# Four images through two attention layers and two Mamba layers: the last MLP of each image, the reload of x, and a softplus one slot later

## The chip, the cores and the metric

One NeuronCore of a Trainium2 chip runs the whole program. The metric is device time in microseconds (us). The kernel before took 12309.68 us in the median of three runs (12303.26 to 12313.59).

The engines are named as in the profile: PE multiplies matrices (PEld loads its weights), DVE and POOL work elementwise, ACT evaluates functions from a loaded table, and SP issues DMAs. Each engine takes its instructions in the order in which they were written and waits for others by semaphores.

## The reference

x is 4 images of 256 channels and 64 x 64 places. Four layers each add their result to x after a group normalisation (32 groups):

```python
x = x + L0(_gn(x))   # gated scan over rows, then window attention
x = x + L1(_gn(x))   # the same with other weights
x = x + L2(_gn(x))   # layer norm, Mamba with 512 inner channels, 16 states
x = x + L3(_gn(x))   # 4 groups of 64 channels, Mamba with 128 inner channels each, MLP, 1x1 convolution
```

What matters here is the end of L3, for every group of 64 channels, and the softplus in L2:

```python
m = _ln(m, ln1_g, ln1_b)                                   # m: output of the Mamba of one group
m = gelu(m @ fc1_w + fc1_b, approximate=False) @ fc2_w + fc2_b
m = m + skip_scale * ch
xo = m.reshape(4, b, N, D).transpose(1, 3, 0, 2).reshape(b, C, H, W)
y = einsum('oc,bchw->bohw', outc_w, xo)                    # then batch norm: scale and bias per channel
return silu(y)
...
delta = softplus(einsum('blr,dr->bld', dt, dt_proj_w) + dt_proj_b)   # in L2's Mamba
```

## The kernel before, in words

`net_kernel` (L1924) runs the images one after the other. For each it takes the x tile (128 partitions, two halves of 4096 columns, 4 MB), loads both halves (L1932), and calls `attention_layers` for L0 and L1, `mamba_layer` for L2 and `grouped_mamba_layer` for L3. x stays in the on-chip memory between the layers. The first thing that L0 does with it is a sum over a strip of eight columns (`gn_s`, L145); a strip has all 64 rows, so it reaches through the whole tile. Before it, DVE prepares small constants from the loaded vectors `att_v` (L107).

Both Mamba layers cut the 4096 places of an image into 4 chunks of 1024 and each chunk into 4 blocks (in L2 128 of the 512 channels, in L3 one group, of which two form a pair c). `scan_blocks` (L800 to L944) goes through all blocks; a block has 16 slots, one per state n. In a slot, DVE multiplies `pb` by `du` (L912) and scans (`h`, L918), POOL multiplies by C (`hc`, L924), ACT makes a later slot's decay (`da`, L854), SP loads a later slot's C row (`cb`, L818, three slots ahead, four buffers), PE spreads a later slot's B row into `pb` (L842) and turns the products of the slot before into the sum `y` (L870). In a few slots (0, 5, 10 in L2; 0, 4, 8 in L3) B comes by DMA instead (`bb`, L824, one buffer), POOL multiplies it by `du` (L828) and the decay goes to PSUM (`dap`). After a block, `end` copies `y` into `du` (L881), turns it back and adds the D term on PE (`fin_ps`, L891, L895), and multiplies by the gate (`m_zs`, L884); this happens in slots 1 to 3 of the next block, and after the last block at once.

All other work is put by hand into slots: `put(block, (slots), steps)` appends steps to a block's slots, and they run on their engines after that slot's scan and products. A slot's place in the code thus sets its order on every engine's queue.

- `x_proj` makes the B, C and step rows of a block (`table_steps`, L1058 to L1090): products on PE, an eviction to `bct` on ACT, two DMAs of B and C rows to memory, and then four correction steps (ACT L1079, POOL L1082, ACT, POOL) which split B for the spreading.
- `delta` makes the softplus of a block (`delta_steps`): `dt_ps` on PE (L1039), Abs, Exp and Ln on ACT (L1041 to L1043), an addition on DVE (L1047), each twice, then `du` on POOL (L1051).
- In L2, these run for the next chunk's first block in the last block of a chunk (L1399, L1400): projections in slots 7, 8, 8, 9, corrections in 9 to 12, softplus in 9, 10, 10, 11 and `du` in 12.
- In L3, `mlp(k, c, s)` (L1633) is the MLP of half s (512 places) of pair c of chunk k, seven steps: output product and its square and copy (L1640 to L1646), variance and inverse root (L1650, L952, L953), multiplication on POOL (L1655), first MLP product (L1661), two Gelus with the second product between, after which ACT's table for Exp and Ln is loaded again (L1668, L948), and the second product with the skip term in two steps (L1684, L1689, L1694). A pair's two halves run in the slots of the next pair; what does not fit goes to the pair after that (`late`).
- `out_conv` (L1709, L1715) makes the 1x1 convolution with the batch norm, `out_silu` (L1728) the Silu of a chunk's four pieces, and `out` (L1734, L1735) adds x on POOL and writes the piece to memory.

After the last scan (L1905 to L1920) the code runs the late steps of pair (3, 0), second half; then both halves of the last pair's MLP, first three steps in turn, then the first half to its end and the second half to its end; then four convolutions, one Silu pass, four additions with four output DMAs. PSUM's pool "mm" has two banks of 512 columns and serves all of these products; the pool "pb" has two buffers of 1024.

The table load for Gelu or Silu is its own ACT instruction, put in where the next function is not in the loaded set.

Of the kernel before, what the change touches and what calls it, by code (L numbers as in the profile page):

```python
# [8 lines left out]
F32 = mybir.dt.float32  # L9
# [9 lines left out]
P = 128  # L19
# [25 lines left out]
class Net:  # L45
# [1067 lines left out]
    def mamba_layer(self, x, bridge, pe_dram, w_in, w_cw, w_x, w_dt, w_out, v_dram):  # L1113
        tc, nc = self.tc, self.nc
        ND = 4
        with ExitStack() as ctx:
# [148 lines left out]
            def delta(k, d):  # L1265
                return self.delta_steps(
                    chunks[k]["blocks"][d], wdt[:, d * P : (d + 1) * P], work, psum
                )
# [76 lines left out]
            for k in range(n_chunk):  # L1345
                more = k + 1 < n_chunk
                bg = [blk["bg"] for blk in chunks[k]["blocks"]]

                def put(d, where, steps):
                    for i, f in zip(where, steps):  # L1350
                        bg[d].setdefault(i, []).append(f)

                if k == 0:
                    put(0, (2, 3, 4, 5), folds)
                if k:
                    for i, where in enumerate(((3, 4, 5), (6, 7, 8), (9, 10, 11), (12, 13, 14))):
                        put(0, where, out_proj(k - 1, i // 2, i % 2))
                put(0, (9, 10, 11, 12, 12), delta(k, 1))
                put(0, (14, 15), (in_z(k, 0, 0), in_z(k, 0, 1)))
                put(1, (1,), (silu((k, 0, "zs")),))  # L1360
                put(1, (6, 7, 8, 9, 10), delta(k, 2))
                put(1, (11, 12), (in_z(k, 1, 0), in_z(k, 1, 1)))
                put(1, (14,), (silu((k, 1, "zs")),))
                at = (6, 7, 8, 9, 10) if more else (5, 6, 7, 8, 9)
                put(2, at, delta(k, 3))
                at = (10, 11) if more else (8, 9)
                put(2, at, (in_z(k, 2, 0), in_z(k, 2, 1)))
                z3 = in_z(k, 3, 0), in_z(k, 3, 1)
                if more:
                    put(3, (0, 1), z3)  # L1370
                else:
                    put(2, (10, 11), z3)
                if more:

                    if k == 0:
                        put(0, (0,), (lambda: begin(1),))
                        put(0, (0, 0, 1, 3, 4, 5, 6, 7), self.later(lambda: norm(1, 0), 8))
                    h1 = self.later(lambda k=k: norm(k + 1, 1), 8)
                    if k:
                        put(0, (2, 4, 5, 7, 8, 13, 14, 15), h1)  # L1380
                    else:
                        put(0, (7, 8, 9, 12, 13, 14, 15), h1[:7])
                        put(1, (1,), h1[7:])
                    if k + 2 < n_chunk:
                        put(3, (3,), (lambda k=k: begin(k + 2),))
                        h0 = self.later(lambda k=k: norm(k + 2, 0), 8)
                        put(3, (4, 6, 7, 14, 15), h0[:5])
                        chunks[k + 1]["late"] = ((0, 1, 2), h0[5:])
                    if k:
                        put(0, *chunks[k]["late"])  # L1390
                    u = all_u(k + 1)
                    put(1, range(5, 16), u[:11])
                    put(2, range(14), u[11:25])
                    put(3, (1, 2, 3, 4, 5, 5, 6), u[25:])
                    xs = x_proj(k + 1)
                    put(2, (13,), (silu((k + 1, 0, "u"), (k + 1, 1, "u"), (k + 1, 2, "u"),
                                        (k, 2, "zs")),))
                    put(3, (7,), (silu((k + 1, 3, "u"), (k, 3, "zs")),))
                    put(3, (7, 8, 8, 9, 9, 10, 11, 12), xs)  # L1399
                    put(3, (9, 10, 10, 11, 12), delta(k + 1, 0))  # L1400
                else:
                    put(2, (13,), (silu((k, 2, "zs"), (k, 3, "zs")),))

                    sums, about, square, squares, early_squares = stats

                    def square_into(i):
                        tag, bufs = ("pe", 1) if i % 2 else ("u", 5)
                        square(i, work.tile([P, NC], F32, tag=tag, name="cs_sq", bufs=bufs))

                    for i in range(6):  # L1410
                        put(1 + (13 + i) // DS, ((13 + i) % DS,), (lambda i=i: sums(i),))
                        put(2 + (12 + i) // DS, ((12 + i) % DS,), (lambda i=i: square_into(i),))
                        put(2 + (13 + i) // DS, ((13 + i) % DS,), (lambda i=i: squares(i),))
                    put(2, (3,), (about,))
                    put(3, (3,), (early_squares,))
                    for i in range(4):
                        at = (6 + 2 * i, 7 + 2 * i)
                        put(3, at, out_proj(k, i // 2, i % 2, ((0, 1, 2),)))
# [67 lines left out]
        return [step(i) for i in range(n)]  # L1486


    def grouped_mamba_layer(self, x, bridge, begun, ws_dram, outc_dram, v_dram, out_b):
        tc, nc = self.tc, self.nc  # L1490
        w_in, w_cw, w_x, w_dt, w_out, w_f1, w_f2 = ws_dram
        with ExitStack() as ctx:
# [209 lines left out]
                )  # L1702


            def out_conv(k, s, m):
                def step():
                    ps = psum.tile([P, NT], F32, tag="mm", name="oc_ps")
                    for c in range(2):
                        nc.tensor.matmul(  # L1709
                            ps, woc[:, c, m * P : (m + 1) * P],  # L1710
                            chunks[k]["xo", c][:, s : s + NT], start=(c == 0), stop=(c == 1),
                        )
                    if s == 0 and m == 0:
                        chunks[k]["yo"] = work.tile([P, 4, NT], F32, tag="hid", name="yo", bufs=1)
                    nc.scalar.activation(  # L1715
                        yo(k, s, m), ps, AF.Identity, bias=bnb[:, m : m + 1], scale=bns[:, m : m + 1]
                    )

                return step
# [7 lines left out]
                for sm in outs:  # L1727
                    nc.scalar.activation(yo(k, *sm), yo(k, *sm), AF.Silu)  # L1728

            def out(k, s, m):  # L1730
                def step():
                    t0 = k * NC + s
                    xs = x[:, m * T + t0 : m * T + t0 + NT]
                    nc.gpsimd.tensor_tensor(yo(k, s, m), xs, yo(k, s, m), ALU.add)  # L1734
                    nc.sync.dma_start(out_b[m * P : (m + 1) * P, t0 : t0 + NT], yo(k, s, m))  # L1735

                return step
# [112 lines left out]
            for i, (k, c) in enumerate(pairs):  # L1850
# [19 lines left out]
                if i:  # L1870
                    m0, m1 = mlp(*pairs[i - 1], 0), mlp(*pairs[i - 1], 1)
                    put(even, (5, 6, 7, 10, 11, 12, 13), m0)
                    put(even, (6, 7, 8), m1)
                    if c == 0:
                        put(even, (14, 15), m1[3:])
                        put(odd, (0, 1), m1[5:])
                    else:
                        put(odd, (15,), m1[3:])
                        late.append(((0, 1, 1), m1[4:]))
                put(even, (7, 8, 8, 9, 10), delta(k, 2 * c + 1))  # L1880
                also = [lambda k=k: out_silu(k - 1)] if c == 1 and k else []
                if i == 0:
# [4 lines left out]
                put(even, (3,), (silu(k, c, "zs", also),))  # L1887
                if c == 1 and k:
                    put(even, (4, 4, 5, 5), [out(k - 1, *sm) for sm in outs])
                if c == 0 and k:  # L1890
                    put(odd, (10, 12, 15), [out_conv(k - 1, *sm) for sm in outs[:3]])
                    late.append(((0,), [out_conv(k - 1, *outs[3])]))
# [9 lines left out]
                [blk for c in chunks for blk in c["blocks"]], loop, psum, psb, psy, (0, 4, 8),  # L1902
                (1, 2, 2), (xs0[2:4], (), xs0[4:]),
            )
            k = n_chunk - 1  # L1905
            for _, steps in late:
                for f in steps:
                    f()
            tail = [mlp(k, 1, 0), mlp(k, 1, 1)]
            for i in range(3):  # L1910
                for fs in tail:
                    fs[i]()
            for fs in tail:
                for f in fs[3:]:
                    f()
            for sm in outs:
                out_conv(k, *sm)()
            out_silu(k)
            for sm in outs:
                out(k, *sm)()  # L1920


@with_exitstack
def net_kernel(ctx, tc, a, out):  # L1924
    net = Net(tc, ctx)
    nc = tc.nc
    xp = ctx.enter_context(tc.tile_pool(name="x", bufs=1))
    x_dram = a["x"]
    for b in range(NB):
        x = xp.tile([P, 2 * T], F32, name="x")  # L1930
        for c in range(2):
            nc.sync.dma_start(x[:, c * T : (c + 1) * T], x_dram[b, c * P : (c + 1) * P, :])  # L1932
        net.attention_layers(
            x, [a[f"l{i}_w"] for i in range(2)], [a[f"l{i}_v"] for i in range(2)]
        )
        with tc.tile_pool(name="bridge", bufs=1, reuse_waits="tile") as bridge:
# [3 lines left out]
            )  # L1940
            net.grouped_mamba_layer(
                x, bridge, begun, [a[f"m3_{k}"] for k in ("in", "cw", "x", "dt", "out", "f1", "f2")],
                a["m3_oc"], a["m3_v"], out[b],
            )


# [81 lines left out]
```

## Time and profile before

| what | us |
|---|---|
| median of three runs | 12309.68 |
| profiled execution, its own time | 12326.55 |
| its span | 12324.8 |
| x loads of the four images issued at | 0.75, 3083.27, 6161.24, 9240.05 |
| image 0: attention, first Mamba, grouped Mamba | about 992, 1039, 1052 |
| busy: PE, DVE, POOL, ACT | 9979.3, 9877.7, 8959.7, 7059.2 |
| granted PE clock, mean over the span | 0.916 |

The profile is of one execution. Its timeline lists instructions with start, duration, engine, line, what they write and read, and in brackets how long the engine stood idle before and who ended that. The chain of waits follows the end back from step to step, and its rows give start, duration and the step; "issue" is time for which no wait is seen. The windows view gives, for a stretch of time, the busy time of PE, PEld, DVE, ACT and POOL (with the number of instructions), then the granted clock of PE (1.00 is full), the share of time in which the DMA engines were busy, and GB/s.

### The profile page before, as it was taken

To read this page: it belongs to the slowest core of one execution; us is meant where nothing else is said; L and a number is where in the kernel's file an instruction comes from. 1 tells how busy PE (TensorE), PEld (TensorE's weight loads), DVE (VectorE), ACT (ScalarE), POOL (GpSimd) and SP (SyncE) were. 2 spreads that over 40 slices of the span, in tenths; PEclk is the share of its full clock that TensorE was granted. 3 is DMA by queue.
4 is the path that set the end of the run, shared out by engine and by line. 5 is a ranking of instruction groups with operands and counts; after the bars stand their busy time and mean duration, and the time that the engine had idled before them with its cause. 6 is when DMAs were issued, how large, how long until landed. Compare 5 with 4: busy or idle time off the path is not lost.

```text
span 12324.8 us, 191425 instructions
## 1 busy us (share of the span) xinstructions
PE 9979.3 (81%) x70976; PEld 5673.2 (46%) x70976; DVE 9877.7 (80%) x8362; ACT 7059.2 (57%) x13044; POOL 8959.7 (73%) x4570
## 2 busy tenths in 40 slices
PE   7887887777788788777788878877778887887777
PEld 4554444443455444444345544444434554444443
DVE  6667998897666799889766679988976667998887
ACT  4555555776455555577545555557754555555775
POOL 3666886887366688688736668868873666886887
PEclk9998998998899899899889989989988998998998
DMA  2344554554334455455433445545542344554554
GB/s 90 103 122 133 168 173 144 168 168 142 93 102 122 133 168 173 144 169 170 141 91 102 123 135 169 172 145 167 170 142 89 102 123 135 169 172 144 167 170 140
DMA packets 680421, 1742.03 MB, mean 141 GB/s; under 512 B 89120, under 2 KB 195120, under 8 KB 678464
## 3 DMA queue, kind: packets, MB, share of 16 engines
q1 hardware_dynamic: 679488, 1729.78, 43.8%
q8 instruction: 562, 9.21, 0.3%
q14 instruction: 371, 3.04, 0.1%
HBM read 1601.51 MB, written 94.37 MB: 138 GB/s over the span
## 4 chain that ended last, share of the span: by engine, by line
DVE 33%; PE 33%; ACT 16%; issue 9%; POOL 6%; DMA 2%; SPq 2%; DVEq 0%; POOLq 0%; ACTq 0%
DVE h L918 16%; PE conv_ps L204 7%; DVE pb L912 7%; PE y L870 5%; PE u_ps L1205 3%; ACT pr L501 3%; ACT da L854 2%; PE pb L842 2%; DVE lp L240 2%; PE sc L480 2%; DVE mn L490 2%; PE u_ps L1572 2%; SPq L456 1%; POOL pr L515 1%; DMA kv<-kv_dram 1%
## 5 line engine op out<-in xcount | busy, mean ns | idle before, releaser
L924 POOL TENSOR_TENSOR hc<-h,cb 128x1024 f32<-128x1024 f32 x2056 | 4815.6, 2351 | 965.0 <-DVE h L918 416.4
L918 DVE TENSOR_TENSOR_SCAN h<-da,m_state,pb 128x1024 f32<-128x1024 f32 x1248 | 2919.8, 2340 | 159.7 <-POOL bb L828 1.0
L870 PE MATMUL y<-ident,hc 128*128 128x128 f32 x16384 | 2371.7, 293 | 345.7 <-POOL hc L924 272.0
L870 PEld LDWEIGHTS y<-ident,hc 128*128 128x128 f32 x16384 | 2093.4, 152 | 1011.6 <-POOL hc L924 447.2
L912 DVE TENSOR_TENSOR pb<-du,pb 128x1024 f32<-128x1024 f32 x1672 | 2024.5, 1211 | 95.6 <-PE pb L842 92.8
L854 ACT ACTIVATE da<-delta,m_v 128x1024 f32<-128x1024 f32 x1672 | 1898.8, 1141 | 221.0 <-DVE h L918 204.2
L842 PE MATMUL pb<-m_parts,pick 128*128 128x512 bf16 x3312 | 1098.1, 416 | 871.4 <-DVE h L918 818.0
L501 ACT ACTIVATE pr<-sc,mn 128x256 f32<-128x256 f32 x2048 | 958.0, 490 | 773.0 <-DVE mn L490 555.3
L515 POOL TENSOR_TENSOR pr<-pr,sm 128x1024 f32<-128x1024 f32 x512 | 967.3, 1899 | 457.8 <-DVE sm L513 359.7
L842 PEld LDWEIGHTS <-pick 128*128 128x128 bf16 x3312 | 255.6, 101 | 1880.0 <-DVE h L918 1155.4
L918 DVE TENSOR_TENSOR_SCAN h<-da,pb 128x1024 f32<-128x1024 f32 x424 | 969.5, 2287 | 54.0 <-DVE pb L912 0.5
L828 POOL TENSOR_TENSOR bb<-du,bb 128x1024 f32<-128x1024 f32 x376 | 889.4, 2365 | 79.7 <-DMA bb<-m_cd 71.3
L490 DVE TENSOR_REDUCE mn<-sc 128x4 f32<-128x1024 f32 x512 | 609.7, 1219 | 386.0 <-PE sc L480 386.0
L529 PE MATMUL pt_ps<-ident,pr 128*128 128x128 f32 x4096 | 592.0, 290 | 219.6 <-ACT pts L542 136.9
L918 DVE TENSOR_TENSOR_SCAN h<-dap,m_state,bb 128x1024 f32<-128x1024 f32 x288 | 672.0, 2333 | 76.1 <-ACT dap L854 63.0
L204 PE MATMUL conv_ps<-att_y,att_wb 128*128 128x512 f32 x1536 | 692.8, 595 | 4.4 <-DVE gn_mean L151 4.4
L529 PEld LDWEIGHTS pt_ps<-ident,pr 128*128 128x128 f32 x4096 | 474.1, 147 | 432.9 <-issue 192.4
L854 ACT ACTIVATE dap<-delta,m_v 128x1024 f32<-128x1024 f32 x376 | 419.5, 1116 | 416.9 <-DVE h L918 318.4
L480 PE MATMUL sc<-kv,q 32*64 32x128 f32 x16384 | 410.5, 300 | 151.5 <-DMA kv<-kv_dram 94.9
L555 PE MATMUL ov_ps<-pts,kv 128*32 128x64 f32 x16384 | 432.4, 234 | 112.4 <-DVE pts L540 65.4
L240 DVE SCALAR_TENSOR_TENSOR lp<-vimg,att_v,lp 128x512 f32<-128x512 f32 x616 | 465.5, 756 | 27.9 <-DVE lp L240 0.5
L859 ACT ACTIVATE m_state<-h 128x1 f32<-128x1 f32 x1536 | 290.6, 192 | 344.2 <-DVE h L918 343.5
(269 smaller groups left out, 17409.3 us busy)
## 6 DMA issues: line engine op xcount, KB each, us to landing
cb<-m_cd SPq DMA_DIRECT2D x2048, 512.0 KB
kv<-kv_dram SPq DMA_DIRECT2D x2048, 128.0 KB
bb<-m_cd SPq DMA_DIRECT2D x376, 512.0 KB
kv_dram<-kst SPq DMA_DIRECT2D x128, 256.0 KB
kv_dram<-vn SPq DMA_DIRECT2D x128, 256.0 KB
q<-q SPq DMA_DIRECT2D x256, 128.0 KB
x<-in_x_dram SPq DMA_DIRECT2D x8, 2048.0 KB
m_pe<-in_pe_dram SPq DMA_DIRECT2D x32, 512.0 KB
```

The costliest lines, as they stand in the source:

```text
L204: nc.tensor.matmul(ps, w[:, k, w0 + m * P : w0 + (m + 1) * P], src[:, k], start=(k == 0), stop=(k == 1),)
L490: nc.vector.tensor_reduce(mn[h], sc[h].rearrange("p r w m n -> p (w m) r n"), AX.XY, ALU.min)
L501: nc.scalar.activation(t[:, g].rearrange("p j r t -> p r j t"), sc[h][:, :, g // 2, g % 2, :].rearrange("p r (j t) -> p r j t", j=2), AF.E ...
L515: nc.gpsimd.tensor_tensor(t, t, s.rearrange("p (a o) -> p a o", o=1).to_broadcast([P, 4, 256]), ALU.mult,)
L529: nc.tensor.transpose(pt[h][j][:, g, :], t[:, g, j].rearrange("p r t -> p (r t)"), self.ident,)
L828: nc.gpsimd.tensor_tensor(pb[i], slots[i][0]["du"], pb[i], ALU.mult)
L842: nc.tensor.matmul(pb[i][:, ss], self.pick[:, n : n + 1].to_broadcast([P, P]), blk["parts"][:, ss], start=True, stop=True,)
L854: nc.scalar.activation(da[i], blk["delta"], AF.Exp, scale=blk["a"](n))
L870: nc.tensor.matmul(blk["y"][:, ss], t[:, ss], self.ident, is_transpose=True, start=(n == 0 and ss.start % NT == 0), stop=(n == DS - 1 and ...
L912: nc.vector.tensor_tensor(pb[i], blk["du"], pb[i], ALU.mult)
L918: nc.vector.tensor_tensor_scan(h[i][:, ss], da[i][:, ss], pb[i][:, ss], state, ALU.mult, ALU.add)
L924: nc.gpsimd.tensor_tensor(hc[i][:, ss], h[i][:, ss], cb[i][:, ss], ALU.mult)
```

## The change

Four things change, in three functions.

1. L2: the four correction steps go from slots 9 to 12 to slots 10 to 13, and the next block's softplus from slots 9, 10, 10, 11 (and 12 for `du`) to 10, 11, 11, 12, 12, and is written ahead of the corrections in a slot they share.
2. L3, last pair: the leftover steps of the second half of pair (3, 0) run in slots 3 to 6 of the last block instead of after the scan.
3. L3, after the scan: both halves of the last MLP go together. All the output products, squares and copies come first, then both inverse roots, with the multiplication on DVE; the first MLP product of both groups goes into one "pb" buffer and one Gelu takes it at 1024 columns; no table load lies between the halves; the Gelus' results go into free buffers of `delta` and `du`. The Silu reads the convolution's PSUM bank directly, with batch norm's scale and bias, and the addition of x is on DVE, piece by piece.
4. x is one tile for all images. Chunk k - 1 of the next image is loaded (1 MB) in slot 8 of the first block of pair (k, 1), after that chunk's output additions in slots 4 and 5; chunk 3 after the last output. Only the first image is still loaded at once.

```diff
-                    put(3, (7, 8, 8, 9, 9, 10, 11, 12), xs)
-                    put(3, (9, 10, 10, 11, 12), delta(k + 1, 0))
+                    put(3, (7, 8, 8, 9), xs)
+                    put(3, (10, 11, 11, 12, 12), delta(k + 1, 0))
+                    put(3, (10, 11, 12, 13), xs[4:])
...
-            def out_conv(k, s, m):
+            def out_conv(k, s, m, func=AF.Identity):
...
-                        yo(k, s, m), ps, AF.Identity, bias=bnb[:, m : m + 1], scale=bns[:, m : m + 1]
+                        yo(k, s, m), ps, func, bias=bnb[:, m : m + 1], scale=bns[:, m : m + 1]
...
-            def out(k, s, m):
+            def out(k, s, m, eng=nc.gpsimd):
...
-                    nc.gpsimd.tensor_tensor(yo(k, s, m), xs, yo(k, s, m), ALU.add)
+                    eng.tensor_tensor(yo(k, s, m), xs, yo(k, s, m), ALU.add)
...
-                    else:
+                    elif i + 1 < len(pairs):
                         put(odd, (15,), m1[3:])
                         late.append(((0, 1, 1), m1[4:]))
+                    else:
+                        put(odd, (3, 4, 5, 6), m1[3:])
...
+                    put(even, (8,), [lambda k=k: load(slice((k - 1) * NC, k * NC))])
...
-            for _, steps in late:
-                for f in steps:
-                    f()
-            tail = [mlp(k, 1, 0), mlp(k, 1, 1)]
...
+            k, pair = n_chunk - 1, chunks[-1]["blocks"][2:]
+            sq = [work.tile([P, 2, NT], F32, tag="sq", name="m_sq") for s in range(2)]
+            for s in range(2):
...
+                nc.scalar.activation(sq[s][:, 0, :], ps, AF.Square)
+                nc.scalar.activation(sq[s][:, 1, :], ps, AF.Copy)
+            for s in range(2):
...
+                self.rsqrt(sq[s][:, 0, :], pv, self.eps)
+                nc.vector.tensor_tensor(sq[s][:, 1, :], sq[s][:, 1, :], sq[s][:, 0, :], ALU.mult)
+            hid = {}
+            for s in range(2):
+                for f in range(2):
+                    ps = psb.tile([P, 2, NT], F32, tag="pb", name="f1_ps")
...
+                    nc.scalar.activation(hid[s, f], ps, AF.Gelu, bias=f1b[:, f : f + 1])
...
+            for s in (0, NT):
+                for m in range(2):
+                    out_conv(k, s, m, AF.Silu)()
+                    out(k, s, m, nc.vector)()
+            load(slice(k * NC, T))
...
+    x = xp.tile([P, 2 * T], F32, name="x")
+
+    def load(b, ts):
+        if b < NB:
+            nc.sync.dma_start(
+                x.rearrange("p (c t) -> p c t", c=2)[:, :, ts], x_dram[b][:, :, ts]
+            )
```

## The prediction

> **What bounds the kernel now.** I read the sum first. The profiled execution took 12326.55 us with a span of 12324.8, and the three timed runs have a median of 12309.68; the sum below is made against the profiled execution and its gain is then taken from the median. The four x loads start at 0.75, 3083.27, 6161.24 and 9240.05 us, so one image takes about 3080 us and every edit is paid four times (the reload three times, the first Mamba layer's shift twelve).
>
> The page's busy shares (PE 81%, DVE 80%, POOL 73%) are averages and say little here, so the next view is the chain of waits over the boundary between image 0 and image 1, in order of time (start, us, what):
>
> ```profile
> 3028.04 2.53 POOL hc L924 x2
> 3030.56 18.29 issue
> 3048.89 1.28 POOL m_sq L1655
> ...
> 3067.99 7.08 PE oc_ps L1709 x16
> ...
> 3075.89 1.28 ACT L1728
> ...
> 3077.89 4.94 POOL yo L1734 x4
> ...
> 3084.24 12.23 DMA att_v<-in_l_v_dram
> 3096.97 2.25 DVE gn_s L145 x2
> ```
>
> The last scan product ends at 3030.57. From there to the x load at 3083.27 lie 52.7 us of small dependent steps, with no other work beside them; then 13.6 us of pure loading until DVE's first reduction at 3096.88. The same stretch is 53.2 us in images 1 and 2 and, up to the last addition, 54.7 us in image 3. So about 66 us per image boundary have one thing running at a time.
>
> Two rows of the timeline show why even the scan's own last step is late. The Gelu of a leftover MLP half takes its table load here, and holds both "mm" banks that the scan's `fin_ps` needs:
>
> ```profile
> 3032.45 1.28 ACT L1668 ACT_TABLE_LOAD   x1
> 3033.74 1.27 ACT L1668 ACTIVATE hid<-f_ps,m_f1b 128x512 f32<-128x512 f32 x2
> 3034.48 0.71 PEld L891 LDWEIGHTS fin_ps<-ident,du 128*128 128x128 f32 x4 [3.45 <-ACT hid L1668]
> ```
>
> The windows view gives PE's busy time first and the granted clock third from last:
>
> ```profile
> 3027.00:3032.00 5.00, 2.40 (x16) 1.69 (x16) 2.18 (x2) 0.64 (x2) 3.37 (x3) 1.00 0.00 2
> 3032.00:3037.00 5.00, 2.52 (x6) 1.48 (x7) 0.00 (x0) 2.99 (x4) 0.00 (x0) 0.50 0.00 0
> 3047.00:3052.00 5.00, 2.59 (x7) 0.60 (x6) 0.00 (x0) 4.72 (x8) 2.50 (x2) 1.00 0.00 0
> 3052.00:3057.00 5.00, 4.89 (x8) 1.59 (x10) 0.00 (x0) 3.30 (x5) 0.00 (x0) 0.55 0.00 0
> ```
>
> Twice PE is half idle for five us, and in the next five its clock is half. In the tail the clock is a cost of its own.
>
> For the first Mamba layer I read DVE's timeline in the last block of the third chunk, and POOL's in that of the second:
>
> ```profile
> 1753.09 2.33 DVE L918 TENSOR_TENSOR_SCAN h<-dap,m_state,bb 128x1024 f32<-128x1024 f32 x1
> 1758.52 0.69 DVE L1047 SCALAR_TENSOR_TENSOR delta<-dt_ps,delta 128x512 f32<-128x512 f32 x1 [3.10 <-ACT delta L1043]
> ```
> ```profile
> 1522.22 2.12 POOL L1082 TENSOR_TENSOR m_bct<-m_bct,m_parts 64x1024 f32<-64x1024 f32 x1
> 1524.31 2.35 POOL L924 TENSOR_TENSOR hc<-h,cb 128x1024 f32<-128x1024 f32 x1
> 1528.13 2.36 POOL L924 TENSOR_TENSOR hc<-h,cb 128x1024 f32<-128x1024 f32 x1 [1.47 <-issue]
> ```
>
> DVE stands still for the softplus: 2.02, 1.86 and 3.10 us at the three chunk ends, 2.04, 1.85 and 3.11 in the other images: 7.0 us per image, 28 in all. POOL idles only 1.45 and 1.47 us in the same stretch of the first two.
>
> **Part 1, the tail.** I rebuild it from the same rows, once with PE at full clock and once at half, starting from 3030.57. In brackets: full / half.
> - The leftover half is gone from here, so `fin_ps` starts when the first `du` copy ends (3031.9, not 3034.5). Transposes and diagonal product twice, then the second 0.69 us multiply: ends 3035.2 / 3037.7 (before 3040.2).
> - `m_ps`, Square and Copy: PE to first Square 1.1 to 2.2, then ACT's four took 2.12 from 3045.16: ends 3037.7 / 3042.1.
> - Ln and Exp for both halves 2.58 (3047.47 to 3050.05); the multiply goes from POOL (1.28) to DVE (0.69 by L1287's and L884's rows) and hides under the Gelu table's 1.28: first Gelu 3041.9 / 3046.5.
> - Four Gelus of 128x1024 instead of eight of 128x512. No row shows this op at that width; L854 of the same size takes 1.14, so four are 4.6, and PE's two 64-row products between them add nothing at full clock (1.16 to the evicting op, row 3050.21) and about 2 in all at half: ends 3046.4 / 3053.2.
> - `f2_ps` twice: from skip product to `xo` 3.07 at full clock (3064.99 to 3068.06), 5.3 at half (3054.69 to 3060.00), the first partly under the last Gelu; `xo` ends 3051.6 / 3060.4.
> - `oc_ps` is paced by PE, 16 matmuls in 7.1. Silu is read from PSUM, so its table load (1.28) fits under PE's first pair, the separate Silu pass (2.19) goes, and the four POOL additions (4.93 on the path) become DVE additions of which only the last 0.69 shows. `oc_ps` starts under the last `xo`, so last addition 7.9 after it at full clock, 8.2 at half.
>
> The x load is then issued at about 3060 / 3069, not 3083.27. PE has no gap above 2.5 us in this tail but is half idle around Ln/Exp, which is what preceded half clock before; I take 3063: 20 us per image in images 0 to 2 and 22 in image 3, where the tail before was 2 longer. **Tail: -83** (ends -57 and -97). Where a stall goes, the next one late is PE: 7.1 us of `oc_ps` and about 6 of `f2_ps`.
>
> By the Trainium skill (ScalarE: Activation LUTs, What ACT_TABLE_LOAD costs) a table switch costs 2.66 us, a load of 1283 ns and a drain of 1380. The rows agree on the load (1.28), but the Gelu after the load at 3061.06 starts at 3062.35, with no drain between; each tail goes from seven loads to two, so by the page's price the tail would gain up to 6.9 us more per image.
>
> **Part 2, x by chunks.** Before, 4 MB and the small `att_v` behind them: 13.3 us from 3083.27 to 3096.60, moved at 358 GB/s by the windows view. 4.2 MB at that rate are 11.7, which leaves 1.6 fixed. Only the last chunk (1 MB, 2.9 us) is still loaded at the boundary: 4.5 by that split. From above, a 512 KB `bb` load issued at 2479.92 was awaited until 2484.77, 4.9 us; another 512 KB at 358 GB/s give 6.3. I take 5. The first strip needs every row of x, so it does wait for this last chunk. **-8.6 three times, -26** (-22 to -28). `att_wa` waits for the last output DMA and then 1 MB; the first convolution starts 11.9 us after the first reduction, which covers it.
>
> The other nine loads sit at slot 8 of an even block, on SP's queue between `cb` loads; the next `bb` load (2479.92) comes only four `cb` loads after it. Queued behind each are `cb` loads for POOL's products. POOL never waited for a `cb` load in this trace, each is issued three slots ahead (some 10 us), and 1 MB takes 2.9. The PE read it waits for is the next chunk's mean, eight slots back. I cost them at nothing; without the cover each costs 2.9, 26 in all; I allow 0 to 9.
>
> **Part 3, the shift.** DVE now does slot 11's product and scan (3.5 us) before the first addition, which swallows the wait. `dt_ps` moves behind a transposition on PE, and ACT's three softplus steps follow, so some 0.4 of the wait stays. Late next is POOL: it does the same work (hc, correction, hc, `du`, hc, correction, `bb` product), and the next block's first scan needs that `bb` product. In the first two chunks it can move up only by its idle 1.45 and 1.47; in the third, where POOL idles 2.85 and 1.80 and DVE then waits 0.74 for `bb`, by 3.1. 6.0 per image, **-24** (0, if a later wait takes it, to -28). The correction's second half ends 3 us later against the `bb` product, but the first block slot that reads it comes after the one that reads `bb`.
>
> **Part 4, the moved MLP half.** Its Gelus and two table loads (5.1 us of ACT) go into slots 3 to 6 of the last block. The half before it sits in slots 10 to 13 of the block ahead (ACT 2957.5 to 2964.2), and DVE waited for nothing from 2952 to 2992; in the last block ACT idles up to 9.5 us at a time. PE is held behind the Gelu for some 3 us, and DVE's next `pb` is due two slots on: I take **+4** in all (0 to 12).
>
> **Sum.** -83 - 26 - 24 + 4 = -129: 12197.6 on the profiled execution, 12181 against the median of 12309.68.
>
> **Rivals.**
> - Full clock: all tails as in the first column, 3 us less each, 12 in all: 12169. The row at 3062 to 3075 has the clock at 1.00 with PE 61 to 100% busy. By the Trainium skill (TensorE: Matmul & The Clock Gate, Part 1) the clock halves only after an idle window of about 3.4 us, and no gap here is that long; the rows speak against it, since 3052 to 3057 ran at 0.55 after gaps of 1.75 and 0.8. Chance 0.15.
> - Half clock throughout: tail -57, 12207. For it 3032 to 3037 and 3052 to 3057; against it that PE, kept busy at half clock, was back at 1.00 by 3062. 0.15.
> - The shift gains nothing, since in the first two chunks POOL and then PE (a 2.10 us wait at 1307.03) set the pace: 12205. 0.10.
> - The boundary load is not shorter, because what is waited for is `att_v`, issued behind it and fixed in time: 12207. Against it: 4 MB at 358 GB/s fill nearly all of the 13.3. 0.03.
> - Slower: an x chunk at the head of SP's queue starves the `cb` loads and with them POOL. Nine loads must give back 129 and 25 more, so 17 us each, which on top of some 10 us of lead means SP held for 27 us, nine times the transfer. 12335. 0.02.
> - The forecast: 0.55.
>
> The range takes in the bounds of the terms: 12157 (tail -97, load -28, shift -28, moved half 0) to 12232 (tail -57, load -22, shift -12, moved half +4, chunk loads +9). About 0.2% (25 us) is what a measurement here can tell from no change. Even the three weak rivals together leave 53 us of gain. Faster 0.97, same 0.01, slower 0.02.
>
> **What would show it.** Last product to x load some 32 us, with one Gelu and one Silu table load and the clock above 0.5 on average; x load to first reduction 5 to 6 us; no wait above 0.6 before L1047 at the three chunk ends, and the block after each starting 1.5, 1.5 and 3 us sooner; no POOL wait for `cb`; the last block's slots still 3.6 us apart. A wait of DVE for `pb` in slots 5 and 6 there, or a tail above 38 us, would make it wrong.

## The result and the profile after

The changed kernel takes **12180.01 us** (median of 4 runs, 12170.0 to 12184.12); the kernel before, timed beside it, 12311.64 (4 runs, 12303.26 to 12316.47). The ratio is 0.9893, with a 95% interval from 0.9875 to 0.9910. The prediction said 12181.

I cut the span of each profiled execution at DVE's own marks: first `gn_s` of an image, first and last scan of L2, first and last scan of L3, next image's first `gn_s` (or the span's end). Sums over four images, in us:

| kernel | span | attention | L2 scans | between | L3 scans | tails with reload |
|---|---|---|---|---|---|---|
| before | 12324.8 | 4145.9 | 3816.4 | 214.8 | 3870.1 | 263.5 |
| after | 12176.8 | 4134.5 | 3791.6 | 213.1 | 3874.2 | 149.4 |

The tails lost 114.1, the L2 scans 24.8, and the L3 scans gained 4.1: 134.8 from code that the change touches. The rest of the two spans' 148 lies in code that is the same: 11.4 in the attention part, which ranges from 4119.8 to 4148.9 over the fourteen profiles of this case, and 1.7 between the scans. Each profile is one execution.

The tail of image 0 on the timeline (start, duration, engine, line, operation, what it writes and reads, idle time ahead); the last scan product, `hc`, ends at 3017.19:

```profile
3018.65 0.66 PE L891 MATMUL fin_ps<-ident,du 128*128 128x128 f32 x4 [0.74 <-ACT du L881]
3027.43 1.28 ACT L1936 ACT_TABLE_LOAD   x1
3028.72 2.12 ACT L1936 ACTIVATE hid_t<-f_ps,m_f1b 128x1024 f32<-128x1024 f32 x2
3037.80 7.13 PE L1711 MATMUL oc_ps<-xo,m_woc 128*128 128x512 f32 x16
3038.62 1.28 ACT L1717 ACT_TABLE_LOAD   x1
3045.78 0.69 DVE L1736 TENSOR_TENSOR yo<-x,yo 128x512 f32<-128x512 f32 x1 [1.02 <-ACT yo L1717]
3046.93 0.39 SPq L1970 DMA_DIRECT2D x<-in_x_dram  x1
3052.80 0.17 DVE L107 TENSOR_SCALAR half_b2b<-att_v 128x2 f32<-128x2 f32 x1 [6.33 <-DMA att_v<-in_l_v_dram]
```

Two table loads are left, one for Gelu and one for Silu; `fin_ps` waits for the `du` copy alone; the Silu's load lies under `oc_ps`. Last product to x load is 29.74 us (31.57, 29.74 in images 1, 2, and 31.59 to the last addition in image 3); x load to first reduction is 6.15, 5.86 and 6.40.

At the three chunk ends of L2 in image 0, the longest wait left is:

```profile
1271.01 0.69 DVE L1047 SCALAR_TENSOR_TENSOR delta<-dt_ps,delta 128x512 f32<-128x512 f32 x1 [0.64 <-ACT delta L1043]
```

It was 2.02 us before; the other two fell from 1.86 to 0.52 and from 3.10 to 0.17.

### The profile page after: what moved, and what is told of

It is laid out like the page before. It is cut to its first block, busy times and chain, and to the rows that moved or that the text cites. A ratio compares the mean times of both kernels' runs of the same rounds, so it can differ in the third digit from the quotient of the medians.

```text
span 12176.8 us, 191411 instructions
## 1 busy us (share of the span) xinstructions
PE 9908.5 (81%) x70976; PEld 5642.1 (46%) x70976; DVE 9896.6 (81%) x8386; ACT 7028.8 (58%) x13000; POOL 8928.9 (73%) x4546
## 4 chain that ended last, share of the span: by engine, by line
DVE 23%; PE 21%; ACT 10%; issue 6%; POOL 4%; DMA 1%; SPq 1%; DVEq 0%; POOLq 0%; ACTq 0%
DVE h L918 13%; DVE pb L912 5%; PE y L870 4%; PE conv_ps L204 4%; PE u_ps L1205 2%; ACT da L854 2%; PE pb L842 1%; ACT pr L501 1%; PE u_ps L1574 1%; DVE lp L240 1%; ACT dap L854 1%; PE z_ps L1230 1%; POOL pr L515 1%; PE sc L480 1%; PE fin_ps L895 1%
## 5 line engine op out<-in xcount | busy, mean ns | idle before, releaser
L828 POOL TENSOR_TENSOR bb<-du,bb 128x1024 f32<-128x1024 f32 x376 | 888.9, 2364 | 68.5 <-DMA bb<-m_cd 62.1
L204 PE MATMUL conv_ps<-att_xn,att_wa 128*128 128x512 f32 x1024 | 463.0, 606 | 14.2 <-POOL att_xn L180 14.2
```

What stands on the lines that cost most here:

```text
L204: nc.tensor.matmul(ps, w[:, k, w0 + m * P : w0 + (m + 1) * P], src[:, k], start=(k == 0), stop=(k == 1),)
L828: nc.gpsimd.tensor_tensor(pb[i], slots[i][0]["du"], pb[i], ALU.mult)
```

## The experiments

My theory was that four independent savings add up. The rivals were that two of them share a gain, that the in-scan loads or POOL take some of it back, and that one piece alone carries the tail. Medians are compared with the kernel before on the same chip (12314 to 12318 there).

| kernel | median | ratio, 95% interval | L2 scans | L3 scans | tails |
|---|---|---|---|---|---|
| shift only | 12282.62 | 0.9973 (0.9963 to 0.9983) | 3791.8 | 3859.9 | 262.0 |
| tail only | 12225.89 | 0.9930 (0.9917 to 0.9944) | 3810.2 | 3867.1 | 172.6 |
| load only | 12289.79 | 0.9981 (0.9972 to 0.9990) | 3818.9 | 3862.1 | 238.2 |
| half after the scan | 12213.68 | 0.9918 (0.9904 to 0.9932) | 3792.7 | 3867.6 | 184.5 |
| old output | 12206.51 | 0.9912 (0.9898 to 0.9925) | 3790.5 | 3874.0 | 176.6 |
| early skip | 12169.00 | 0.9881 (0.9866 to 0.9896) | 3795.9 | 3864.8 | 141.8 |
| shift in L3 | 12167.56 | 0.9880 (0.9865 to 0.9895) | 3792.7 | 3849.7 | 151.2 |
| split load | 12166.02 | 0.9884 (0.9869 to 0.9899) | 3797.1 | 3864.4 | 142.8 |
| these three | 12160.60 | 0.9878 (0.9861 to 0.9894) | 3792.5 | 3849.0 | 134.4 |
| and later corrections | 12134.14 | 0.9855 (0.9838 to 0.9871) | 3794.8 | 3832.0 | 134.3 |
| idle products | 12174.87 | 0.9890 (0.9874 to 0.9907) | 3795.2 | 3866.1 | 157.4 |
| all with idle products | 12134.94 | 0.9856 (0.9840 to 0.9873) | 3790.9 | 3834.4 | 140.8 |

**One part at a time.** Each of the first three is the kernel before with one part of the change.

```diff
-                    put(3, (7, 8, 8, 9, 9, 10, 11, 12), xs)
-                    put(3, (9, 10, 10, 11, 12), delta(k + 1, 0))
+                    put(3, (7, 8, 8, 9), xs)
+                    put(3, (10, 11, 11, 12, 12), delta(k + 1, 0))
+                    put(3, (10, 11, 12, 13), xs[4:])
```

> The kernel before with one part of the change: the first Mamba layer's softplus in its last blocks one slot later, and the four corrections of its x_proj behind it. Theory (the parts are independent, and the shift gives what the profile of after shows in that layer's scan): each image's L2 scan goes from 954 to 948 us, the three waits before L1047 from 2.02/1.86/3.10 us to about 0.6 or none, the whole 24 to 25 us less than before, ratio 0.998. Rival (the gain is handed on to POOL, whose idle time at the first two chunk ends was only 1.45 us, or it appeared only together with the other parts): the scan stays at 954 us, ratio 1.000, with waits for POOL in the block after.

The L2 scans lost 24.6 us, as with all parts together, and DVE's waits for POOL did not grow there. The rival falls.

The tail alone has the new code behind the scan, with the other half in slots 3 to 6 of the last block, and loads x at the image's start as before:

> The kernel before with one part of the change: the last MLP with both halves together, SiLU from PSUM, the adds on VectorE, and the other half moved into slots 3 to 6 of the last block; x is loaded at the image's start as before, the softplus is where it was. Theory (a chain shortened by its own length): last product to x load falls from 53 to about 30 us in images 0 to 2 and from 55 to 32 in image 3, 91 us in all, the last scan takes 1 us more per image; 87 less than before, ratio 0.9929; the time from the x load to the first reduction stays at 13.6 to 14 us. Rival (tail and load are not additive: with the output pieces issued closer together, the 2 MB load behind them runs against them and takes longer, 17 us rather than 14): 75 to 78 less, ratio 0.9938.

The tails lost 90.9. From x load to first reduction it is 13.48, 14.09 and 13.71 us, so the old load does not stretch. The load alone has one x tile and the chunk loads of the change:

> The kernel before with one part of the change: one x tile for all images, the next image's first three chunks loaded by SyncE during the second scan, only the last chunk behind the tail. Theory: from the last chunk's load to the first reduction 6 us instead of 13.6 to 14, three times, 23 less, ratio 0.9981; nothing in the scans (no wait for cb or bb). Rival 1 (the nine in-scan loads delay the broadcasts of cb and bb behind them on SyncE's queue by up to a microsecond each): 12 to 23 us come back and it is the same as before within 10. Rival 2 (the reduction waits for att_v, queued behind x, and not for x itself, so the load's length is not what counts): less than 10 us gained.

The tails lost 25.3, and the reload is 6.81, 6.01 and 6.71 us long. DVE's first instruction after the boundary waits for `att_v` in both, here first the tail alone (x load at 3057.49), then the load alone (x load at 3067.46):

```profile
3070.68 0.17 DVE L107 TENSOR_SCALAR half_b2b<-att_v 128x2 f32<-128x2 f32 x1 [13.65 <-DMA att_v<-in_l_v_dram]
```
```profile
3073.99 0.17 DVE L107 TENSOR_SCALAR half_b2b<-att_v 128x2 f32<-128x2 f32 x1 [49.61 <-DMA att_v<-in_l_v_dram]
```

`att_v` arrives 13.2 us after the x load was issued in one and 6.5 in the other: what it waits for is the amount queued ahead of it. Neither rival holds: POOL's waits for `bb` loads came to 65.3 us over the whole run (71.3 before, 62.1 after), and no idle time of POOL, here or in after, ends with a `cb` load. The three parts give 24.6 + 90.9 + 25.3 = 140.8 in their stretches, and together 24.8 + 114.1 = 138.9. In these stretches they add. The medians are coarser: the three fell by 33.3, 90.0 and 26.1, 149.4 in all, against 131.6 together, and their intervals reach 11 to 22 us to either side.

**Pieces of the tail, undone in the changed kernel.** First the leftover half runs behind the scan again:

```diff
-                    elif i + 1 < len(pairs):
+                    else:
                         put(odd, (15,), m1[3:])
                         late.append(((0, 1, 1), m1[4:]))
-                    else:
-                        put(odd, (3, 4, 5, 6), m1[3:])
...
+            for _, steps in late:
+                for f in steps:
+                    f()
             k, pair = n_chunk - 1, chunks[-1]["blocks"][2:]
```

> The changed kernel with one piece undone: the first half of the last MLP's column (the leftover of the earlier pair) runs its fc1, Gelu and fc2 behind the scan again, ahead of the new tail, and not in slots 3 to 6 of the last block. Theory (in the tail each table load, Gelu and product group is on the path; in the scan the same work costs 1 us per image): last product to x load 5 to 9 us longer per image, 20 to 36 in all, less the 4 that leave the scan, so 16 to 32 more than the changed kernel, 12,196 to 12,212. Rival (the leftover runs beside the end of the last block's products, where ScalarE waits 3.4 us for TensorE anyway): within 4 us of the changed kernel.

The tails grew by 35.1 and the L3 scans fell by 6.6. The old row is back (`hc` ends at 3016.69 here):

```profile
3019.87 1.26 ACT L1670 ACTIVATE hid<-f_ps,m_f1b 128x512 f32<-128x512 f32 x2
3020.61 1.12 PE L891 MATMUL fin_ps<-ident,du 128*128 128x128 f32 x4 [3.21 <-ACT hid L1670]
```

`fin_ps` starts 3.92 us after the last product in all four images, as in the kernel before; without the half it is 1.45 to 1.91. So the leftover half does not run beside the scan's end, it holds it up. The larger part of the 35 us comes after that: from `fin_ps` to the first Square it is 10.24 to 11.33 us in this run and 3.87 to 5.74 without the half, whose second group of products, Gelu and table load stand in between. The second piece undone is the output: Identity, a Silu pass, POOL's additions.

```diff
-            for s in (0, NT):
-                for m in range(2):
-                    out_conv(k, s, m, AF.Silu)()
-                    out(k, s, m, nc.vector)()
+            for sm in outs:
+                out_conv(k, *sm)()
+            out_silu(k)
+            for sm in outs:
+                out(k, *sm)()
```

> The changed kernel with one piece undone: the output's batch norm goes to Identity, a separate pass of four SiLU follows, and the four adds run on POOL, as before. Theory (what follows the last product is all on the path): one Identity of 0.78 us ends where the last SiLU ends now, then a table load of 1.28, four SiLU of 0.78, and the last POOL add of 1.27 in place of VectorE's 0.69; 5 to 7 us more per image, 20 to 28 in all, 12,200 to 12,208. Rival (the SiLU and the adds of the first pieces were hidden under the 7.1 us of TensorE's last 16 products and the outputs' own transfers hide the rest): less than 8 us in all.

The tails grew by 27.2. The Silu pass comes whole after the last product, and POOL's last addition ends 3.4 us after it:

```profile
3040.09 2.19 ACT L1730 ACTIVATE yo<-yo 128x512 f32<-128x512 f32 x4
3040.79 4.92 POOL L1736 TENSOR_TENSOR yo<-x,yo 128x512 f32<-128x512 f32 x4 [30.57 <-ACT yo L1730]
```

If the pieces add, 35 of the 91 us of tail are the leftover half and 27 the output; what is left, about 29, goes with running both halves together (fewer table loads, wider Gelus). That last share was not run by itself.

**Does PE set the new tail?**

```diff
+                if s == 0:
+                    skip_product(0)
                 for f in range(2):
...
                     nc.scalar.activation(hid[s, f], ps, AF.Gelu, bias=f1b[:, f : f + 1])
+                if s == 0:
+                    skip_product(1)
```

> The changed kernel with the two skip products of 1.06 us ahead of the hidden layer's sums: one issued before fc1's products, where TensorE waits 1.19 us for VectorE, the other between the two halves of fc1, where it waits 0.95 us for ScalarE; nothing else is moved. Theory (from the last Gelu on, TensorE is what sets the tail's end, so what is issued earlier leaves the path): last product to x load 1.8 to 2.1 us shorter, 7 to 8 in all. Rival (ScalarE's Gelu and table loads set it; TensorE's time lies beside them): within 1 us per image of the changed kernel.

Where the clock is full from the start (images 1 and 3 there), last product to x load is 27.48 us, against 29.74: 2.3 shorter. In the other two it is 29.30 and 29.75, against 31.57: about 2 shorter. The theory holds in the profile; the median alone could not show it.

**The same shift where there is more to shift.**

```diff
-                    put(odd, (8, 8, 8, 9, 10, 11), x_proj(nk, 2 * ncol))
-                    put(odd, (9, 10, 10, 11, 12), delta(nk, 2 * ncol))
+                    xs = x_proj(nk, 2 * ncol)
+                    put(odd, (8, 8), xs[:2])
+                    put(odd, (10, 11, 11, 12, 12), delta(nk, 2 * ncol))
+                    put(odd, (10, 11, 12, 13), xs[2:])
...
-                put(even, (7, 8, 8, 9, 10), delta(k, 2 * c + 1))
+                put(even, (8, 9, 9, 10, 10), delta(k, 2 * c + 1))
```

> The changed kernel with the same shift in the second Mamba layer: in odd blocks the softplus in slots 10 to 12 rather than 9 to 12 with the four corrections of x_proj in 10 to 13, in even blocks the softplus one slot later. Theory (a wait of VectorE for ScalarE's softplus is worth what it lasts wherever another slot hides it; L1047 waits 34.8 us in 22 waits in one image's scan there, and in the first layer a fifth to a third of each wait stayed): the second scan falls from 968 to between 940 and 950 us per image, 70 to 110 in all, 12,070 to 12,110. Rival 1 (there the next wait is as long: VectorE waits next for dap from ScalarE, 13 us, or for pb from TensorE, 15 us, because it is the same backlog that is late): the waits change their name and the scan stays at 965 to 970. Rival 2 (POOL gets du so late that its products are late at each block's start): slower, up to 2 us per block, 15 blocks, 4 images, 12,300.

My theory failed here. The L3 scans fell by 24.5 us against the changed kernel, not by 70 to 110 (and by 18.7 against the mean of the six profiles with the same L3 schedule, which range from 3864.4 to 3874.2). The groups of DVE in the L3 scan of image 0 (busy us, mean ns, then idle us ahead of them and who ended it), first of after, then of this run:

```profile
L1047 DVE SCALAR_TENSOR_TENSOR delta<-dt_ps,delta 128x512 f32<-128x512 f32 x32 | 21.9, 685 | 34.8 <-ACT delta L1043 34.8
L978 DVE TENSOR_TENSOR m_xn<-x,ln_pm 128x1024 f32<-128x1024 f32 x6 | 7.2, 1201 | 0.3 <-PE ln_pm L975 0.3
```
```profile
L1047 DVE SCALAR_TENSOR_TENSOR delta<-dt_ps,delta 128x512 f32<-128x512 f32 x32 | 21.5, 674 | 16.9 <-ACT delta L1043 16.9
L978 DVE TENSOR_TENSOR m_xn<-x,ln_pm 128x1024 f32<-128x1024 f32 x6 | 7.3, 1210 | 6.1 <-PE ln_pm L975 6.1
```

Half of the waits stayed, all in even blocks. Of the 17 us per image that went, 11 came back as other waits of DVE: L978 (the centring of the next chunk's norm) for PE (5.4), the `bb` scans for POOL (3.4), `pb` for PE (2.0). DVE's idle time in the scan fell by 5.8 per image, which is the 6.1 that the scan lost. In L2 the same shift took 5.2 of wait per image and DVE's idle time fell by 6.1: there, on balance, nothing came back. So this is mostly rival 1.

**The last chunk in two halves.**

```diff
             for s in (0, NT):
...
+                load(slice(k * NC + s, k * NC + s + NT))
-            load(slice(k * NC, T))
```

> The changed kernel with the last chunk of the next image's x loaded in two halves, the first issued as soon as the first two output pieces are out and the second behind the last two. Theory (the 1 MB load behind the tail is bound by the transfer: 6.1 us from issue to first reduction at 0.99 of the DMA engines' time): 1.5 to 3 us less per boundary, three boundaries, 5 to 9 in all. Rival (the reduction waits for att_v, which is queued behind x and is on the way with the output pieces, or the halves only change the order in which the same bytes go): within 1 us per boundary.

From the last load's issue to the first reduction it is 5.48, 5.03 and 4.97 us, 0.7, 0.8 and 1.4 less, 2.9 in all. The rest of the tails' 6.6 is the clock: all four tails happened to start at or near full clock here (29.3 to 29.7 us from the last product to the last addition). The rival is nearer than the theory.

**All three, and a second cause removed.** The run with all three together:

> The changed kernel with the three additions of the three runs before together: skip products early, the last x chunk in two halves, the softplus of the second Mamba layer one slot later. Theory (the three lie in different stretches and add up): tails 7.6 and 6.6 us shorter, scans 17 to 24, from the stretches measured one by one; 31 to 38 less than the changed kernel, 12,142 to 12,149, ratio 0.986. Rival (the halves of the load start while TensorE's last products run, and the tail that is shorter by 2 us leaves less time to hide the first half, so the two overlap): 5 us less of it, 12,150 to 12,155.

Its stretches are as short as expected (tails 15.0 less than in the changed kernel, L3 scans 25.2 less), but its median is 12160.6, not 12142 to 12149. For the tails that is in part luck: the 6.6 us expected of the split load held 3.7 of clock, and here three tails of four ran at full clock (3.87 us from `fin_ps` to the first Square) against two in the changed kernel; the reload itself took 4.54, 4.35 and 5.09 us. In its profiled execution (span 12153.8) the attention part took 11.2 and the stretch between the scans 5.2 more than in that of after; why they vary stays open. The next run adds:

```diff
-                put(even, (4, 5, 6, 7, 8, 9), x_proj(k, 2 * c + 1))
+                xs = x_proj(k, 2 * c + 1)
+                put(even, (4, 5), xs[:2])
+                put(even, (10, 11, 12, 13), xs[2:])
...
-                    put(even, (0, 1, 4, 5, 6), h0)
+                    put(even, (0, 2, 4, 5, 6), h0)
```

> As the run with all three, and in the second Mamba layer's even blocks the four corrections of x_proj behind the softplus too (slots 10 to 13 rather than 6 to 9), and the centring of the next chunk's norm one slot later (slot 2). Theory (in the shifted kernel the softplus of even blocks, 8 waits of 2.1 us per image, waits for POOL's correction of bct ahead of it, 2202.52 to 2204.65 us in the first image, since TensorE's dt product starts when that ends): these waits go, and those before L978 (5.7 us per image); if all of it stays in the scan's end, 20 us per image less, 80 in all, 12,065; if a third stays as in the odd blocks, 7 per image, 28 in all, 12,117. Rival (POOL's later corrections collide with du, in slot 10 there, and the next block's first products wait for POOL): the waits change their name to POOL and the time is that of the run with all three or up to 30 us over it.

Most of the waits at L1047 went, as the cause named in the expectation says, and those at L978 too; the two moves were not run apart. DVE then waits for `pb` twice as long as in the changed kernel (16.2 there):

```profile
L912 DVE TENSOR_TENSOR pb<-du,pb 128x1024 f32<-128x1024 f32 x209 | 253.3, 1212 | 33.0 <-PE pb L842 19.9 <-PE f_ps L1663 9.1 <-remote 3.5
...
L1047 DVE SCALAR_TENSOR_TENSOR delta<-dt_ps,delta 128x512 f32<-128x512 f32 x32 | 21.4, 670 | 3.6 <-ACT delta L1043 3.6
```

Per image, about 26 us of waits went against the run with the shift alone, and 21 came back, the `bb` scans' waits for POOL (3.2) among them; the L3 scans are 17.0 shorter than with all three, and the median is 26.5 lower, where 28 were expected if a third stayed. With 12134.14 us this is the lowest median, 0.9855 of the kernel before, and its interval lies below that of the changed kernel.

**The clock in the tail.** In the changed kernel the first steps of the tail take longer in images 1 and 3: from `fin_ps` to the first Square 5.24 and 5.73 us, against 3.87 in images 0 and 2. This run puts idle products ahead:

```diff
+            def warm():
+                ps = psum.tile([P, NT], F32, tag="mm", name="warm_ps")
+                for _ in range(3):
+                    nc.tensor.matmul(
+                        ps, skip, chunks[-1]["xn"][:, 1, 3 : 3 + NT], start=True, stop=True
+                    )
+
+            put(odd, (14, 15), (warm, warm))
```

(and `warm` before the last transposes).

> The changed kernel with nine idle products of TensorE in the last two slots of each image's last scan (three ahead of each of the last three groups of transposes, into a tile that nothing reads). It tests whether the tails' length goes by the granted clock: in images 0 and 2 the clock is back at 1.00 when the last products start and 29.74 us lie between the last product of the scan and the x load; in images 1 and 3 it is 0.50 to 0.68 for the first six us and they take 31.57 and 31.59. Theory: with TensorE busy in the slots ahead the clock is granted before the scan ends, and all four tails take 29.5 to 30 us, 3.6 us less in all. Rival 1 (the clock follows what TensorE does in a longer stretch, and nine products don't change it): two tails still take 31.5. Rival 2 (the idle products stand ahead of the last transposes and delay them): 1 to 2 us longer in each image.

In the windows view (PE's busy time first, the granted clock third from last) the stretch from `fin_ps` to the first Square in image 1, in after and then here:

```profile
6055.80:6061.00 5.20, 5.20 (x18) 2.58 (x20) 1.39 (x2) 0.39 (x1) 0.00 (x0) 0.73 0.00 0
```
```profile
6053.70:6057.50 3.80, 3.80 (x18) 1.82 (x20) 1.39 (x2) 0.40 (x1) 0.00 (x0) 1.00 0.00 0
```

All four images take 3.87 us for it now, at clock 1.00. But the products, 2.74 us for each three, stand ahead of the last transposes: `fin_ps` starts 3.82, 3.82, 5.95 and 3.82 us after the last product. The tails came out 8.0 longer. So the clock's part of my theory and rival 2 both hold. The fastest version with the same products:

> The kernel of the last run (all three additions, corrections behind the softplus, centring a slot later) with the nine idle products. Theory (the tail is a part by itself): its tails are those of that kernel less up to 1.8 us where the clock was not yet granted; 12,130 to 12,136, ratio 0.985 to 0.986. Rival: the idle products cost 1 us per image, 12,138.

Its tails are 6.5 longer than without, 1.6 per image, so there the rival holds; the median does not tell the two apart. There was nothing to gain: without the idle products all four tails of that kernel's profile already ran at full clock (3.87 us from `fin_ps` to the first Square).

## Why the prediction was right

- **Part 1, tail.** The step that was off is the choice between the two columns, "I take 3063". The full-clock column was right nearly row by row: it put the first Gelu 11.3 us after the last product, the last `xo` 21.0 and the x load 29.4; measured in image 0 are 11.53, 21.42 and 29.74. The tails gave 91 instead of 83. I had expected half clock after the half idle stretch around Ln and Exp; there PE was busy enough (2.22 and 2.46 us of 3.41, last section). What I left out is that the tail can begin at half clock, as it did in images 1 and 3.
- **Part 2, load.** The mechanism held. The term was mis-sized by about one us: 6.15, 5.86 and 6.40 us, not 5. That is 23 us instead of 26. The 358 GB/s came from a window (3082 to 3097) that begins before the old load; over that load's own 13.3 us the view gives 371, but over the new one only 290 to 307. The last output piece (256 KB, issued 0.43 us ahead of the load in image 0) lands 1.83 us after the load's issue, the weight loads queue behind it, and how much of the extra us each makes is not shown. The nine in-scan loads cost nothing that shows: no wait for `cb`, and 3862.1 for the L3 scans of the load alone, against 3870.1 before.
- **Part 3, shift.** 24.8 us against 24, and the limit was the one named, POOL: in the first two chunks its idle 1.45 and 1.47 are gone, and it works from 1273.72 and from 1513.06 on without a pause until the `bb` product is done. The estimate that 0.4 of a wait stays fits 0.64, 0.52 and 0.17, though the first is just above the 0.6 named as the limit.
- **Part 4, moved half.** +4.1 against +4 for the whole L3 scans says little: profiles with the half in the scan have 3864.4 to 3874.2 (six, mean 3868.4), those without 3859.9 to 3870.1 (four, mean 3864.9). The last block alone says more. From its first scan to its last it takes 55.0 us in all four images before, and 56.31, 55.01, 56.25 and 55.54 after: +3.1 in all. DVE waits for `pb` there, in image 0 ahead of the products of slots 5 and 6:

```profile
2976.94 1.23 DVE L912 TENSOR_TENSOR pb<-du,pb 128x1024 f32<-128x1024 f32 x1 [0.88 <-PE pb L842]
2980.84 1.23 DVE L912 TENSOR_TENSOR pb<-du,pb 128x1024 f32<-128x1024 f32 x1 [0.21 <-PE pb L842]
```

That is the wait which the prediction named as a sign of being wrong. It came in three images of four, and was short enough for the 4 us set aside.
- **Rivals.** The shift gave its gain and the boundary load did get shorter (both shown alone). The starved `cb` queue did not occur. Of full clock (12169), half came true: two tails of four ran wholly at it.
- **The sum.** By the profiles the changed code gave 134.8 and not 129, by the medians 131.6. The tail gave 8 more than I said and the load 3 less. That 12181 and 12180.01 lie one us apart is luck: these misses partly cancel, and the four runs themselves spread over 14 us.

## What to carry to other kernels

Where work runs one thing at a time, rebuild the chain from rows of the same operations and add it up; it comes out within a few tenths of a microsecond, and what is left is the clock. Where engines work beside each other, a wait is worth what the next wait leaves of it: the same shift kept all of its gain where three waits stood alone with slack on POOL, and about a third where twenty stood between engines that were equally late. Look for such spare room before pricing a wait at its length.

## What the runs showed of the hardware

The granted clock changes on a fixed grid: all 549 changes in the profile of after lie on steps of 3.413 us. Windows of one us, with 1.00 and 0.50 as the only levels, place the ends of the low stretches in after at 3013.90 and 3017.32 (one step of 3.42 us) and 6051.76 and 6058.60 (two steps); from 3017.32 to 6051.76 it is 889 steps of 3.413. The Trainium skill (TensorE: Matmul & The Clock Gate, Part 1) gives a free-running window of 3413 ns, which agrees. It also says that the clock falls after an idle window, and here the rows differ: PE was partly busy in the step before each fall shown here. Cut on the grid, after in image 0 (ahead of the fall, half clock, and the two leanest steps of its tail):

```profile
3010.49:3013.90 3.41, 1.09 (x8) 0.86 (x8) 3.28 (x3) 0.00 (x0) 2.16 (x2) 1.00 0.00 0
3013.90:3017.32 3.42, 2.80 (x13) 2.50 (x14) 1.90 (x2) 0.00 (x0) 3.09 (x3) 0.50 0.01 2
...
3024.15:3027.56 3.41, 2.22 (x8) 0.68 (x8) 0.81 (x2) 3.09 (x6) 0.00 (x0) 1.00 0.00 0
3027.56:3030.97 3.41, 2.46 (x14) 0.69 (x10) 0.57 (x1) 3.27 (x3) 0.00 (x0) 1.00 0.00 0
```

and before, ahead of its two falls:

```profile
3028.60:3032.02 3.42, 1.70 (x12) 0.99 (x10) 0.62 (x1) 0.66 (x2) 1.96 (x2) 1.00 0.00 0
...
3049.08:3052.50 3.42, 1.52 (x5) 0.60 (x6) 0.00 (x0) 3.35 (x5) 2.31 (x2) 1.00 0.00 0
```

Steps with 1.09, 1.52 and 1.70 us of PE work were followed by half clock, steps with 2.22 and 2.46 were not. Over the whole profile of after, cut the same way, this is sharp only at the ends. Of its steps at full clock, all 146 with less than 1.25 us of PE work were followed by half clock, 112 of 297 with 1.25 to 2 us, 15 of 621 with 2 to 2.75 us, and none of 1878 with more. At half clock, none of 163 steps with less than 2.25 us was followed by full clock, and 199 of 233 with 3.25 us or more were.

Since the grid does not follow the program, the same scan end falls on it differently in each image; that explains why tails of the same code take 29.7 or 31.6 us: in after the fall comes 3.3 us before the last product in images 0 and 2, and 2.1 and 1.1 us before it in images 1 and 3. What ends a low stretch stays open beyond these counts: one step with 2.80 us of work was enough at 3017.32, while 3.42 us of it from 3052.50 in the kernel before were not.
